# Two moves in GpSimd's hand-written order: one fold of each attention unit, and the addition to the sum over heads

## The chip, the cores and the metric

The kernel runs on one core of one Trainium2 chip. The metric is the device time of one execution in microseconds (us). Before the change three runs took 1590.33, 1591.95 and 1596.36 us; their median is 1591.95 us.

## What is computed

Two residual blocks over x of shape (2, 2048, 256), all in float32: first a layer norm and a recurrent network over the 2048 positions, then a layer norm and an attention with 8 heads of width 64, whose values and outputs are mixed from 5 experts by top-2 gates.

```python
x = x + rnn(layernorm(x))                       # h = tanh(x Wi + bi + h Wh + bh)
y = layernorm(x)
q, k = (y @ Wq), (y @ Wk)                       # 8 heads of 64
gl_v = (y @ Ws).reshape(b, t, h, e)
wv = topk_mask(gl_v, 2) * sigmoid(gl_v)
v = einsum('bthe,btek->bhtk', wv, einsum('btd,edk->btek', y, Wv))
probs = softmax(q * scale @ k^T)                # over 2048 keys
attn = einsum('bhij,bhjd->bihd', probs, v)
mask_o = topk_mask((y @ Wd).reshape(b, t, h, e), 2)
out = x + einsum('bthe,bthk,ekd->btd', mask_o, attn, Wo)
```

The last sum runs over heads and experts: each head adds its masked result to a sum `yd` in DRAM, and the product with Wo is made once for all heads.

## The kernel before

The first 190 us hold the recurrent block and the first layer norms. The rest is the attention, one long pipeline whose instruction order is written out by hand: it stands in a region of manual schedule, where each engine does its instructions in the order in which the Python code issues them.

The work is cut into 64 *units*: 2 batches x 8 heads x 4 blocks of 512 queries. A unit has eight tiles of keys, numbered 0 to 7 (variable `c`); a tile is 128 partitions (keys) x 2 x 512 (two groups of 128 keys by 512 queries), 512 KB. The main loop runs over 256 steps `T`; a unit takes `U_T` = 4 steps, two tiles each. A tile goes through these functions:

- `scores` (L636, TensorE): keys by queries into PSUM.
- `stage` (L648, ScalarE): copies the tile from PSUM to a buffer `p` of a ring; `largest` (L658, VectorE) takes the running maximum. The maximum over a unit's keys is turned, reduced and spread again (L677, L682, L691; `top`, L697).
- `subtract` (L704): subtracts that maximum, in place. Tiles 0 and 1 of a unit are done by VectorE, tiles 2 to 7 by GpSimd. It comes `LAG - 1` = 5 steps behind the scores.
- `exponential` (L707, ScalarE), in place. Of a step's two tiles one comes at the end of a step and the other at the start of the next.
- `products` (L717, TensorE): the tile by the values, into `o`, in step `T` for the tiles whose scores were made six steps before.
- `fold` (L729): a DMA that GpSimd issues and that adds the odd tile of a pair to the even one (`accum_op` add). It comes one step after the pair's products. It waits for these products, since it overwrites the even tile, and for the exponentials. A unit has four: of tiles 0, 2, 4 and 6.
- `sums` (L738, TensorE): adds up folded tiles against a column of ones, for the softmax's divisor. In step `T` with `T - LAG` odd; one call takes the folded tiles 0 and 2, the other, two steps later, 4 and 6. It is queued on TensorE behind the products of its step and ahead of the next step's scores.

When a unit is done, `take` and `take_sums` copy and add its results, `close` (L783, VectorE) makes `pro`, the unit's result for the five experts, and `gather` (L829 to L840) adds it to the sum over heads: for head 0 a store by SyncE (L835), for heads 1 to 6 a DMA with addition that GpSimd issues (L837), for head 7 an addition on GpSimd to a tile `y` that was loaded (L840). `pro` has one buffer.

What doesn't belong to the tiles of a step is put into tables by step, `before`, `first_behind` and `behind` (L939 to L1025). In the main loop (L1127 to L1173) a step issues, in this order: `take` and the exponential of an older tile, two score tiles with their staging and maxima, the subtractions and the fold, what `before` holds, the products, the sums, an exponential, and what `behind` holds. GpSimd's own order over a unit's four steps is thus:

- step with `T % 4 == 0`: subtract 6, fold of tile 2, subtract 7
- step with `T % 4 == 1`: fold of tile 4, and `gather` of an older unit (from `behind`)
- step with `T % 4 == 2`: subtract 2, fold of tile 6, subtract 3
- step with `T % 4 == 3`: subtract 4, fold of tile 0, subtract 5

`close` of the same older unit is in `behind` one step ahead of `gather`. SyncE issues the other transfers of the attention: among them the fetch of 640 KB of expert values for the next head (L608), the exchange of query halves (L170, L171), and in parts of the run loads of x, y and z.

Of the kernel before, what the change touches and what calls it, by code (L numbers as in the profile page):

```python
# [20 lines left out]
def rnn_then_switchhead_kernel(  # L21
# [16 lines left out]
    B, T, D = x.shape  # L38
    E, _, DH = Wv.shape
    H = Wq.shape[1] // DH  # L40
# [516 lines left out]
    U_T = NCH // 4  # L557
    LAG = U_T + 2
# [70 lines left out]
    def scores(t):  # L629
        i, n = units[t // HC]  # L630
        c = t % HC
        ss = ps_s.tile([P, 2, QB], F32, tag="s", name=f"s{t}")
        for o in range(2):
            half = slice(o * DH, (o + 1) * DH)
            for g in range(0, P, 32):
                nc.tensor.matmul(  # L636
                    ss[g : g + 32, o, :],
                    lhsT=k_of[i][half, c, g : g + 32],
                    rhs=q_of[i, n][o][half, :],
                    start=True,  # L640
                    stop=True,
                    tile_position=(o * DH, g),
                )
        return ss

    def stage(t, ss):
        p = ap.tile([P, 2, QB], F32, tag=f"p{t % 2}", bufs=RING[t % 2], name=f"p{t}")
        nc.scalar.copy(p, ss)  # L648
        ring[t] = p

    def largest(t, ss):

        u, c = t // HC, t % HC
        if c == 1:
            m_of[u] = ap.tile([P, 2, QB], F32, tag="mx", bufs=1, name=f"m{u}")
        m = m_of[u]
        if c != HC - 2:
            nc.vector.tensor_tensor(m, ss, ring[t - 1] if c == 1 else m, ALU.max)  # L658
            return
        half = misc([P, QB], f"mh{u}")  # L660
        nc.vector.tensor_tensor(half, ss[:, 0, :], m[:, 0, :], ALU.max)
        nc.vector.tensor_tensor(m[:, 1, :], ss[:, 1, :], m[:, 1, :], ALU.max)
        mm_of[u] = ap.tile([P, QB], F32, tag="mm", bufs=1, name=f"mm{u}")
        nc.vector.tensor_tensor(mm_of[u], half, m[:, 1, :], ALU.max)
        m_of.pop(u)
# [7 lines left out]
    def turn_max(u):  # L673
        pm = misc([P, QS, P], f"pm{u}")
        mm = mm_of.pop(u)
        for s in range(QS):
            nc.tensor.transpose(pm[:, s, :], mm[:, s * P : (s + 1) * P], ident)  # L677
        mx_of[u] = (pm, ap.tile([P, QS], F32, tag="mq", name=f"mq{u}"))

    def reduce_max(u):  # L680
        pm, mq = mx_of[u]
        nc.vector.tensor_reduce(mq, pm, AX.X, ALU.max)  # L682
# [16 lines left out]
    def subtract(t, on_vector=False):  # L699
        u, c = t // HC, t % HC  # L700
        p = ring[t]
        on_vector |= c < 2
        eng, top = (nc.vector, top_of[u][0]) if on_vector else (nc.gpsimd, top_of[u][1])
        eng.tensor_tensor(p, p, top.unsqueeze(1).to_broadcast([P, 2, QB]), ALU.subtract)  # L704

    def exponential(t):
        nc.scalar.activation(ring[t], ring[t], AF.Exp)  # L707

    def products(t):
        u, c = t // HC, t % HC  # L710
        i, _ = units[u]
        if c == 0:
            o_of[u] = ps_o.tile([P, QB], F32, tag="o", name=f"o{u}")
        for o in range(2):
            for g in range(0, DH, 32):
                at_col = o * DH + g
                nc.tensor.matmul(  # L717
                    o_of[u][at_col : at_col + 32, :],
                    lhsT=v_of[i][:, 2 * c + o, g : g + 32],
                    rhs=ring[t][:, o, :],  # L720
                    start=c == 0,
                    stop=c == HC - 1,
                    tile_position=(0, at_col),
                )

    def fold(t):


        nc.gpsimd.dma_start(out=ring[t], in_=ring.pop(t + 1), accum_op=ALU.add)  # L729

    def sums(t, t1, first, last):


        u = t // HC
        if first:
            den_of[u] = ps_o.tile([P, QB], F32, tag="d", name=f"d{u}")
        for g in range(4):
            nc.tensor.matmul(  # L738
                den_of[u][32 * g : 32 * (g + 1), :],
                lhsT=ones32,  # L740
                rhs=ring[(t, t1)[g // 2]][:, g % 2, :],
                start=first,
                stop=last,
                tile_position=(0, 32 * g),
            )
        ring.pop(t)
        ring.pop(t1)

    def take(u):

        o = o_of.pop(u)
        os = ap.tile([P, QB], F32, tag="os", bufs=1, name=f"os{u}")
        nc.scalar.copy(os[0:DH, :], o[0:DH, :])
        nc.vector.tensor_tensor(os[0:DH, :], o[DH:P, :], os[0:DH, :], ALU.add)  # L754
        o_of["s", u] = os
# [183 lines left out]
    before, first_behind, behind = {}, {}, {}  # L939

    def at(table, T, f, *a):
        table.setdefault(T, []).append(lambda: f(*a))
# [9 lines left out]
    for i, (b, h) in enumerate(heads):  # L952
# [11 lines left out]
        for part in range(4):  # L964
# [3 lines left out]
            else:  # L968
                T = T0 + U_T * (part - 2) + 2
# [3 lines left out]
        if h == H - 3 and b + 1 < B:  # L973
            for c in range(NCH):
                T = T0 + c // 2 * U_T + 1
                at(before if c % 2 else behind, T + c % 2, experts, b + 1, c)
    for b in range(1, B):

        T0 = (b - 1) * H * H_T + 2 * LAG + 3
        for c in range(NCH):  # L980
            T = T0 + c // 2 * U_T
# [6 lines left out]
        for c in range(NCH):  # L988
            T = T0 + c // 2 * U_T + c % 2
# [12 lines left out]
    for u, (i, n) in enumerate(units):  # L1002
        b, h = heads[i]
        T1 = (u + 1) * U_T
        if T1 < NT:
            at(first_behind, T1, spread_max, u)
        outs = [(b, n * QS + s) for s in range(QS)]
        if T1 + LAG < NT and h == H - 1:
            at(behind, T1 + LAG, fetch_y, u)
        if T1 + LAG + 1 < NT - 1:  # L1010
            at(behind, T1 + LAG + 1, take_sums, u)
            at(behind, T1 + LAG + 2, close, u)
            at(behind, T1 + LAG + 3, gather, u)
        if h == H - 1 and n < NQ - 3:
            T = T1 + LAG + 4
            for o, t, p in zip(outs, (0, 1, 3, 3), (1, 2, 3, 4)):
                if T + t < NT:
                    at(before if o[1] % QS == 2 else behind, T + t, turn_out, *o)
                if T + p < NT:
                    at(behind if o[1] % QS == 2 else before, T + p, project_out, *o)  # L1020
        if h == H - 1 and b < B - 1 and n >= NQ - 3:
            T = T1 + LAG + 4
            for o, t, p in zip(outs, (0, 1, 3, 3), (1, 2, 3, 4)):
                at(before if o[1] % QS == 2 else behind, T + t, turn_out, *o)
                at(behind if o[1] % QS == 2 else before, T + p, project_out, *o)  # L1025
# [100 lines left out]
    with tc.manual_schedule():  # L1126
        for T in range(NT):  # L1127
            new = (2 * T, 2 * T + 1)
            sub = [t for t in (2 * (T - LAG + 1), 2 * (T - LAG + 1) + 1) if 0 <= t < 2 * NT]
            old = [t for t in (2 * (T - LAG), 2 * (T - LAG) + 1) if 0 <= t < 2 * NT]  # L1130
            u_old = (T - LAG) // U_T - 1
            done = (T - LAG) % U_T == 0 and 0 <= u_old < len(units)
            fresh = sub and sub[0] % HC == 0
            if done:
                take(u_old)
            if old:
                exponential(old[1])

            ss = [scores(t) for t in new]
            stage(new[0], ss[0])  # L1140
            if T % U_T == 0:
                stage(new[1], ss[1])
                if T > 0:
                    turn_max(T // U_T - 1)
                    reduce_max(T // U_T - 1)
                largest(new[1], ss[1])
            else:
                largest(new[1], ss[1])
                stage(new[1], ss[1])
            if fresh:  # L1150
                subtract(sub[0])
            if T % U_T:
                largest(new[0], ss[0])
            if fresh:
                subtract(sub[1])
            if sub and not fresh:
                subtract(sub[0])
            k = T - LAG
            if k > 0:
                fold(2 * (k - 1))  # L1160
            if sub and not fresh:
                subtract(sub[1])
            for f in before.pop(T, []):
                f()
            for t in old:
                products(t)
            if 3 <= k and k % 2:
                t = 2 * (k - 3)
                sums(t, t + 2, t % HC == 0, t % HC != 0)
            if sub:  # L1170
                exponential(sub[0])
            for f in first_behind.pop(T, []) + behind.pop(T, []):
                f()  # L1173
        assert not before and not behind and not first_behind
        scores_only.close()
        spare["pool"] = ctx.enter_context(tc.tile_pool(name="ps_z", bufs=4, space=PSUM))
        drain()
# [46 lines left out]
```

## Time and profile before

| | |
|---|---|
| median of three runs | 1591.95 us |
| the profiled execution's own time | 1591.29 us |
| its span in the profile | 1589.5 us |
| TensorE clock granted | 0.996 |
| DMA moved | 254.09 MB, of it 164.65 MB by GpSimd's queue |
| fold DMAs (L729) | 254, 512 KB each, 6.6 us (median) from issue to landing |
| additions to yd by GpSimd (L837) | 48, 640 KB each, 7.6 us |
| fetches xq (L608) | 60, 640 KB each, 5.8 us |

Times in the profile are microseconds from the span's start. A group of instructions reads: line, engine, operation, output and input tile with shapes, count, then total busy time and the mean in ns of one, then the engine's idle time just ahead of the group and what ended most of it. A line of the waits reads: waiting engine, tile and line, what it waited for, then total, number of times, longest. PE is TensorE's matmuls, PEld its weight loads, DVE VectorE, ACT ScalarE, POOL GpSimd, SP SyncE. A line of the timeline reads: start, duration, instruction, count, and in brackets the idle time ahead of it with what ended it.

### The profile page before, as it was taken

What the parts mean: (1) busy time and instruction counts of PE and PEld (TensorE: products, weight loads), DVE (VectorE), ACT (ScalarE), POOL (GpSimd) and SP (SyncE); (2) the same over time, 40 slices, a digit from 0 to 9 for tenths busy, and PEclk for the clock granted to TensorE, in tenths of its full rate; (3) what the DMA queues carried; (4) which work ended last, traced back from release to release, by engine and by line L of the source; (5) the groups of instructions that cost most, each with busy time, mean ns of one, the idle gap of its engine ahead of it and who ended that gap; (6) DMA issues with size and microseconds to landing.
All of it is one profiled execution on the core that took longest, in us unless ns stands there. A gap on an engine that the chain in (4) does not pass through costs nothing. (4 is left out here: it accounts for less than half of the span.)

```text
span 1589.5 us, 41502 instructions
## 1 busy us (share of the span) xinstructions
PE 1529.4 (96%) x17582; PEld 542.1 (34%) x17582; DVE 1299.2 (82%) x1811; ACT 1248.1 (79%) x1617; POOL 1280.7 (81%) x855
## 2 busy tenths in 40 slices
PE   6989899999999999999999999999999999999997
PEld 5984222222233333333223332222222222222233
DVE  7473799999988878888987779989888888898883
ACT  4674688888888878888877678888888888888872
POOL 3053699888889987999997678898889889888880
PEclk9999999999999999999999999999999999999999
DMA  5021368898888888788886667888888888888855
GB/s 164 1 108 31 107 149 184 183 191 179 180 169 176 175 181 172 159 176 179 167 198 148 158 157 179 174 175 178 172 171 170 175 168 163 174 174 178 182 119 151
DMA packets 86959, 254.09 MB, mean 160 GB/s; under 512 B 11952, under 2 KB 31216, under 8 KB 86768
## 3 DMA queue, kind: packets, MB, share of 16 engines
q0 software_dynamic: 43488, 164.65, 55.5%
q1 hardware_dynamic: 41648, 86.13, 17.6%
q8 instruction: 139, 2.28, 0.6%
q10 hardware_dynamic: 1632, 0.61, 0.1%
q14 instruction: 52, 0.43, 0.1%
HBM read 59.46 MB, written 50.33 MB: 69 GB/s over the span
## 5 line engine op out<-in xcount | busy, mean ns | idle before, releaser
L704 POOL TENSOR_TENSOR p<-p,top 128x1024 f32<-128x1024 f32 x378 | 1051.4, 3017 | 10.7 <-ACT top L697 10.7
L648 ACT COPY p<-s 128x1024 f32<-128x1024 f32 x512 | 511.2, 1012 | 155.2 <-DVE m L658 63.3
L707 ACT ACTIVATE p<-p 128x1024 f32<-128x1024 f32 x512 | 538.5, 1063 | 51.3 <-DVE p L704 40.8
L636 PE MATMUL s<-q,k 64*32 64x512 f32 x4096 | 497.5, 596 | 2.8 <-ACT p L648 2.4
L636 PE MATMUL s<-qs,k 64*32 64x512 f32 x4096 | 497.3, 596 | 2.9 <-ACT p L648 1.9
L717 PE MATMUL o<-p,v 128*32 128x512 f32 x4096 | 491.1, 597 | 2.4 <-DVE os L754 1.5
L658 DVE TENSOR_TENSOR m<-s,m 128x1024 f32<-128x1024 f32 x320 | 390.5, 1220 | 108.0 <-PE s L636 99.6
L729 POOL DMA_DIRECT2D p<-p x254 | 346.2, 1364 | 53.3 <-ACT p L707 19.8
L717 PEld LDWEIGHTS o<-p,v 128*32 128x32 f32 x4096 | 113.7, 109 | 298.5 <-issue 157.2
L738 PE MATMUL d<-p,ones 128*32 128x512 f32 x1032 | 156.1, 594 | 8.6 <-DMA p<-p 8.6
L636 PEld LDWEIGHTS s<-qs,k 64*32 64x32 f32 x4096 | 102.6, 106 | 151.5 <-issue 56.7
L636 PEld LDWEIGHTS s<-q,k 64*32 64x32 f32 x4096 | 102.6, 106 | 147.8 <-issue 59.2
L704 DVE TENSOR_TENSOR p<-p,pt 128x1024 f32<-128x1024 f32 x126 | 152.3, 1209 | 0.0
L658 DVE TENSOR_TENSOR m<-s,p 128x1024 f32<-128x1024 f32 x64 | 78.4, 1224 | 57.3 <-ACT p L648 56.8
L837 POOL DMA_DIRECT2D yd<-pro x48 | 44.7, 931 | 90.0 <-DVE pro L783 87.8
L783 DVE TENSOR_TENSOR pro<-po,mr 128x1280 f32<-128x1280 f32 (+1 forms) x67 | 95.9, 1431 | 2.7
L620 DVE TENSOR_TENSOR xq<-xq,wp 128x1280 f32<-128x1280 f32 x60 | 89.2, 1487 | 2.3 <-DVE wp L618 0.3
L626 DVE TENSOR_REDUCE v<-xq 128x256 f32<-128x1280 f32 x60 | 88.6, 1476 | 0.0
L738 PEld LDWEIGHTS d<-p,ones 128*32 128x32 f32 x1032 | 38.0, 110 | 102.6 <-issue 74.8
L159 PE MATMUL pq<-xn2T,wq 128*32 128x512 f32 x512 | 63.2, 612 | 6.3 <-DVE rootd L425 6.3
L140 PE MATMUL pk<-xn2T,wk 128*32 128x512 f32 x512 | 61.5, 598 | 0.0
L396 POOL TENSOR_TENSOR x<-x,hvb 128x512 f32<-128x512 f32 x14 | 17.9, 1277 | 45.8 <-ACT hs L369 34.2
(179 smaller groups left out, 1511.0 us busy)
## 6 DMA issues: line engine op xcount, KB each, us to landing
p<-p POOLq DMA_DIRECT2D x254, 512.0 KB, 6.6
xq<-xvd SPq DMA_DIRECT2D x60, 640.0 KB, 5.8
yd<-pro POOLq DMA_DIRECT2D x48, 640.0 KB, 7.6
qs<-q SPq DMA_DIRECT2D x64, 128.0 KB, 3.3
yd<-pro SPq DMA_DIRECT2D x8, 640.0 KB, 5.3
y<-yd SPq DMA_DIRECT2D x8, 640.0 KB, 7.7
x<-in_x SPq DMA_DIRECT2D x16, 256.0 KB, 5.7
x1d<-x SPq DMA_DIRECT2D x16, 256.0 KB, 2.0
```

The source lines that it names most:

```text
L159: nc.tensor.matmul(pq[at_col : at_col + 32, :], lhsT=wq[:, kc, h * DH + g : h * DH + g + 32], rhs=xn2T[:, kc, b, n * QB : (n + 1) * QB], s ...
L620: nc.vector.tensor_tensor(xq, xq, wp.unsqueeze(2).to_broadcast([P, 4, DH, E]), ALU.mult)
L626: nc.vector.tensor_reduce(v_of[i][:, 4 * part : 4 * part + 4, :], xq, AX.X, ALU.add)
L636: nc.tensor.matmul(ss[g : g + 32, o, :], lhsT=k_of[i][half, c, g : g + 32], rhs=q_of[i, n][o][half, :], start=True, stop=True, tile_positi ...
L648: nc.scalar.copy(p, ss)
L658: nc.vector.tensor_tensor(m, ss, ring[t - 1] if c == 1 else m, ALU.max)
L704: eng.tensor_tensor(p, p, top.unsqueeze(1).to_broadcast([P, 2, QB]), ALU.subtract)
L707: nc.scalar.activation(ring[t], ring[t], AF.Exp)
L717: nc.tensor.matmul(o_of[u][at_col : at_col + 32, :], lhsT=v_of[i][:, 2 * c + o, g : g + 32], rhs=ring[t][:, o, :], start=c == 0, stop=c == ...
L729: nc.gpsimd.dma_start(out=ring[t], in_=ring.pop(t + 1), accum_op=ALU.add)
L738: nc.tensor.matmul(den_of[u][32 * g : 32 * (g + 1), :], lhsT=ones32, rhs=ring[(t, t1)[g // 2]][:, g % 2, :], start=first, stop=last, tile_ ...
L783: nc.vector.tensor_tensor(dst, po[:, s : s + n, 0:DH].unsqueeze(2).to_broadcast([P, n, E, DH]), mr[:, s : s + n].unsqueeze(3).to_broadcast ...
```

## The change

The diff touches two places. In the tables, `gather` of every head but the last is put one step later, into the step with `T % 4 == 2`, where it comes behind that step's two subtractions and its fold. In the main loop, in steps with `T % 4 == 0`, the fold (of tile 2) is issued ahead of both subtractions and not between them. Other steps keep their order.

```diff
         if T1 + LAG + 1 < NT - 1:
             at(behind, T1 + LAG + 1, take_sums, u)
             at(behind, T1 + LAG + 2, close, u)
-            at(behind, T1 + LAG + 3, gather, u)
+            at(behind, T1 + LAG + 3 + (h < H - 1), gather, u)
...
             if fresh:
                 subtract(sub[1])
+            k = T - LAG
+            first = T % U_T == 0
+            if first and k > 0:
+                fold(2 * (k - 1))
             if sub and not fresh:
                 subtract(sub[0])
-            k = T - LAG
-            if k > 0:
+            if not first and k > 0:
                 fold(2 * (k - 1))
             if sub and not fresh:
                 subtract(sub[1])
```

GpSimd's order over a unit's four steps becomes:

- `T % 4 == 0`: fold of tile 2, subtract 6, subtract 7
- `T % 4 == 1`: fold of tile 4 (and `gather` if the older unit is of head 7)
- `T % 4 == 2`: subtract 2, fold of tile 6, subtract 3, `gather`
- `T % 4 == 3`: subtract 4, fold of tile 0, subtract 5

The first move concerns 62 folds, the second the `gather` of 56 units: 48 DMAs of GpSimd and 8 stores of SyncE. The orders of TensorE, VectorE and ScalarE are the same as before. SyncE's eight stores of head 0 come behind the loads and query exchanges of the step that they are moved to.

## The prediction

> **What bounds the kernel now.** I read the page's busy shares first, then the groups, the list of waits, and the timelines of two neighbouring units on TensorE and on GpSimd (POOL). A unit is four steps; its key tiles are 0 to 7. I write S2 to S7 for the six subtractions that GpSimd does (L704), F0, F2, F4, F6 for its four fold DMAs (L729), G for the addition to the sum over heads (L837, a DMA).
>
> ```profile
> PE 1529.4 (96%) x17582; PEld 542.1 (34%) x17582; DVE 1299.2 (82%) x1811; ACT 1248.1 (79%) x1617; POOL 1280.7 (81%) x855
> ...
> L704 POOL TENSOR_TENSOR p<-p,top 128x1024 f32<-128x1024 f32 x378 | 1051.4, 3017 | 10.7 <-ACT top L697 10.7
> ...
> L729 POOL DMA_DIRECT2D p<-p x254 | 346.2, 1364 | 53.3 <-ACT p L707 19.8
> ...
> L738 PE MATMUL d<-p,ones 128*32 128x512 f32 x1032 | 156.1, 594 | 8.6 <-DMA p<-p 8.6
> ...
> L837 POOL DMA_DIRECT2D yd<-pro x48 | 44.7, 931 | 90.0 <-DVE pro L783 87.8
> ```
>
> TensorE is the bound, with nearly no idle time; GpSimd's one regular idle time is ahead of G. The waits add what the group of the sums hides:
>
> ```profile
> POOL yd L837 <- DVE pro L783: 87.8, 42, 3.3
> ...
> PEld d L738 <- DMA p<-p: 27.3, 34, 3.8
> ...
> PE d L738 <- DMA p<-p: 8.6, 7, 2.9
> ```
>
> 34 times TensorE's weight loads for the sums wait for a fold to land: 27.3 us, and the matmuls queued behind wait with them. The timeline of TensorE shows one unit with the wait and the next without it:
>
> ```profile
> 1124.93 1.03 PE L738 MATMUL d<-p,ones 128*32 128x512 f32 x4
> 1126.99 1.05 PE L738 MATMUL d<-p,ones 128*32 128x512 f32 x4 [1.03 <-DMA p<-p]
> 1127.97 0.63 PE L636 MATMUL s<-q,k 64*32 64x512 f32 x4
> ...
> 1146.97 1.04 PE L738 MATMUL d<-p,ones 128*32 128x512 f32 x8
> 1147.95 0.63 PE L636 MATMUL s<-qs,k 64*32 64x512 f32 x4
> ```
>
> With the wait, the first sums of a unit last 3.1 us (1124.93 to 1128.04), without it 1.04. These are the sums of tiles 0 to 3, and the later half needs F2. Reading the start of each unit's first L636 matmul in the trace, the unit with the wait is 22.03 us long and the next 20.29. In the second batch (26 units, 34 to 59), 11 units have no wait and last 20.29 or 20.30; the other 15 last 20.41 to 22.63. A unit's length is 20.29 plus its wait less about 0.32: the maximum of L658 in that step ends 0.3 us later than the sums would, and the next scores wait for that too. The excess over 20.29 adds up to 12.5 us.
>
> GpSimd's timeline over a unit boundary (step 0 of the new unit begins at 1158.31):
>
> ```profile
> 1154.24 1.47 POOL L729 DMA_DIRECT2D p<-p  x1
> 1154.85 5.63 POOL L704 TENSOR_TENSOR p<-p,top 128x1024 f32<-128x1024 f32 x2
> 1159.57 1.76 POOL L729 DMA_DIRECT2D p<-p  x1
> 1160.18 3.56 POOL L704 TENSOR_TENSOR p<-p,top 128x1024 f32<-128x1024 f32 x1
> 1162.51 2.07 POOL L729 DMA_DIRECT2D p<-p  x1
> 1166.27 0.87 POOL L837 DMA_DIRECT2D yd<-pro  x1 [1.69 <-DVE pro L783]
> ```
>
> These are F0, S5 and S6, F2, S7, F4, G. F2 is issued at 1159.57, though its last condition (the products of tiles 2 and 3, ended 1157.5) was met 2 us before: S6 stands ahead of it. Lastly the landing of single folds (DMA issues of L729 in narrow windows), for the F2 of the unit with the wait and of the one without:
>
> ```profile
> DMA to landing us min/median/max: 9.7/9.7/9.7
> ...
> DMA to landing us min/median/max: 5.6/5.6/5.6
> ```
>
> The first was issued at 1117.23, 1.0 us ahead of SyncE's fetch of 640 KB (L608, 1118.20), the second at 1138.54, 1.7 us ahead of it (1140.24).
>
> **What the Trainium skill says.** "Perfetto Trace Analysis", Identifying the Most-Contended Engine: matmul busy time does not tell how near TensorE is to its limit. The trace agrees: PE shows 8.6 us of idle time ahead of the sums, the unit lengths 12.5 us in one batch alone. The same page, DMA Instruction — SWDGE (GPSIMD): a GpSimd DMA's record ends when descriptors are generated, not when data is there. It agrees: record 1.8 us, landing 9.7. "DMA: Bandwidth & Descriptors", Two DMAs through the same engine are not ordered: within one queue descriptors start in order; and its Queues, rings and completion order: an engine alternates between queues packet by packet. So F2 waits for what GpSimd issued before it, and shares with SyncE's transfers from then on; the two landings fit.
>
> **The change part by part.** Instructions, durations and the orders of TensorE, VectorE and ScalarE stay.
>
> F2 ahead of S6, 62 times. GpSimd gives S6 and S7 0.61 us less time early (from F2's start to the next start, 1159.57 to 1160.18) and gets it back before S7. New order here: F2 waits for the products, 1157.2 to 1157.5 (folds start up to 0.3 us before the modelled end of the products), instead of 1159.57: 2.1 to 2.4 us earlier. The added wait holds S6 and S7. S6 then starts at 1158.1 at most (before: 1157.2) and takes 3.0: ends 1161.1; ScalarE takes it 4.26 us into the unit, 1162.6. Cover 1.5 us. S7 starts 2.36 later (S6 follows S5 by that in the trace, as no DMA stands between), 1160.5, ends 1163.5 to 1163.8; it ended 1163.74 before, and its exponential starts at 1164.0. Cost nothing, with 0.2 to 0.5 us of cover, and 1.3 us more (median of the trace) from that exponential's end to its product on TensorE.
>
> F2's landing. SyncE's fetch would now follow 3 us behind F2, not 1 to 1.7, so I take 5.6 us: landed at 1163. With the bad 9.7 it lands at 1167.1; the later half of the sums wants it at 9.5 us into the unit, 1167.8. The wait goes either way.
>
> G behind S2, F6, S3, 48 times (head 7's addition, L840, stays where it is). Its wait (1.9 us a unit, 87.8 in all) is gone, since pro is long done by then; GpSimd was ahead by that much, so this is not 87.8 us of time. It buys S2 to S5 an earlier start, and so F2's issue never slips past the products as it did in units 24 and 28 (S5 ended 0.8 and 2.2 us after the unit began; in 28 this cost 1.4 us of TensorE through S7). It adds 0.57 us ahead of S4, whose exponential comes 3.8 us after S4's end (median): covered. The next pro needs the buffer some 15 us after the new G; G lands in 7.6 (median). The eight stores of head 0 (L835) move on SyncE's queue the same way, past loads that are wanted two steps or more later: nothing.
>
> The GpSimd queue's order becomes F4, F6, G, F0, F2. Issue times in the 20.29 us unit before, from its start (1138.01): F4 4.1, G 8.0, F6 10.9, F0 16.2, F2 21.6, next F4 24.5, gaps from 2.9 to 5.4. After, each fold at the end of its products: F4 4.2, F6 8.9, G 12 (behind S3), F0 15.5, F2 19.3, next F4 24.5, gaps from 3.1 to 5.2, and F2 no longer has the next F4 2.9 us behind it. Unproven is F2 with G and F0 in front: low cost nothing, high a landing of 11 us or more. I take none, as G and F0 have 7 us to pass before F2 is issued.
>
> Sum: second batch 12.5 us; first batch 13 units with waits of 11.4 us in all, 7.3 if each is discounted 0.32; the longest ones (1.97, 3.90) show in full in the unit's length, so 9; unit 28 1.4. Together 22.9, less 1.5 for the 3.90, where two fetches of 640 KB stand beside F2 and some wait stays: 21.5. Against the profiled execution: 1591.3 (span 1589.5 and 1.8 around it) to 1569.8; it stands 0.7 under the median of 1591.95, so 1570.5 as a median. What is late next is L658's maximum in the same step: already in the 0.32.
>
> **The rivals.** Partly: in the first batch other work (experts, gates) fills the same place, and only the second gains, 1591.95 - 12.5 = 1579.5. For: units there last 20.7 to 24 us. Against: their waits show in full. No gain: G and F0 ahead in the queue delay F2's data by as much as it is earlier (2.3 us), 1592. For: the DMA engines are 83% busy in these stretches. Against: the gaps above. Slower, at the same place: F2's landing takes over 10.7 us (0.9 earlier than the unit's start, 9.5 into it, 0.3 of cover); each us beyond costs about 60 units x 1 us, against today's 22, so it decides from 11.1 us; at 11.5 it is 48 - 22 = 26 us, 1618. For: single folds took 12.3. Against: F2's median is 7.3 today, in the same traffic.
>
> **How the numbers follow.** Forecast 0.68 (1563 to 1577), partly 0.15, no gain 0.11, slower 0.06. Range 1563 to 1584: forecast and nearly all of partly. 0.5% (8 us) is what a measurement can tell from no change: below 1584 0.82, within 0.12, above 0.06.
>
> **What would show it.** The wait of the sums for p<-p falls from 27.3 to under 5 us, units of the second batch last 20.3, POOL's wait for pro is gone and waits of L729 for the products appear. Wrong: waits for p<-p as before with a later landing, or ScalarE waiting for L704.

## The result, and the profile after

The changed kernel takes 1570.73 us (median of 6 runs, 1568.86 to 1573.80); six runs of the kernel before have a median of 1593.18 us. The ratio is 0.986, 95% interval 0.984 to 0.988. The profiled execution's span fell from 1589.5 to 1567.6 us.

The page after, for the busy shares and the groups that were shown of before:

```profile
PE 1512.6 (96%) x17582; PEld 533.7 (34%) x17582; DVE 1299.1 (83%) x1811; ACT 1247.8 (80%) x1617; POOL 1287.7 (82%) x855
...
L704 POOL TENSOR_TENSOR p<-p,top 128x1024 f32<-128x1024 f32 x378 | 1006.3, 2768 | 27.9 <-ACT top L697 27.4
...
L729 POOL DMA_DIRECT2D p<-p x254 | 263.0, 1036 | 97.6 <-issue 42.4
...
L738 PE MATMUL d<-p,ones 128*32 128x512 f32 x1032 | 135.0, 592 | 0.9 <-DMA p<-p 0.9
...
L837 POOL DMA_DIRECT2D yd<-pro x48 | 61.0, 1270 | 0.0
```

Busy time of VectorE and ScalarE is what it was. The sums (L738) have lost 21 us, from 156.1 to 135.0, though no matmul was taken out, and the mean record stayed at 592 to 594 ns. The records of the eight matmuls lie over one another when nothing waits (x8 in 1.04 us, in the prediction's lines); when the later four wait for F2, they come as two halves of 1.03 and 1.05 us, one behind the other. So part of a wait shows as busy time. The addition to yd (L837) has lost its idle time of 90.0 us; GpSimd now idles ahead of subtractions (27.9 us, for the maximum) and of folds (97.6 us, where it was 53.3). It is idle in other places, and is not what got faster.

Who waits for a fold, from the profile's view of line 729 (waiting engine, us, times):

```profile
  PEld d L738: 1.8, 1
  PE d L738: 0.9, 1
...
DMA to landing us min/median/max: 4.5/5.4/11.9
```

27.3 us in 34 waits have become 1.8 in one. A fold lands 5.4 us after its issue (median), before 6.6. GpSimd's timeline over the same unit boundary as in the prediction (here the unit begins at 1146.10):

```profile
1137.60 1.21 POOL L837 DMA_DIRECT2D yd<-pro  x1
1138.23 3.01 POOL L704 TENSOR_TENSOR p<-p,top 128x1024 f32<-128x1024 f32 x1
1141.29 0.88 POOL L729 DMA_DIRECT2D p<-p  x1
1141.90 2.70 POOL L704 TENSOR_TENSOR p<-p,top 128x1024 f32<-128x1024 f32 x1
1145.02 0.88 POOL L729 DMA_DIRECT2D p<-p  x1 [0.42 <-issue]
1145.64 5.02 POOL L704 TENSOR_TENSOR p<-p,top 128x1024 f32<-128x1024 f32 x2
1150.32 1.18 POOL L729 DMA_DIRECT2D p<-p  x1
```

These are G, S4, F0, S5, F2, S6 and S7, F4. F2 is issued 1.08 us ahead of the unit; before it was 1.26 behind. The 0.42 us ahead of it, named "issue", is the wait for the products: 57 of the 64 folds of tile 2 start 0.27 to 0.29 us before their modelled end.

Unit lengths, from the first L636 matmul of each unit (a unit is numbered here by the sums that fall into it, and begins with the first scores of the next unit but one): in the second batch, 25 of 26 units last 20.30 or 20.31 us (before: 20.29 to 22.63). Both batches were added up against the kernel before: the 26 units of the second are 12.6 us shorter, the 34 of the first 8.4. That is 21.0 of the span's 21.9; the rest lies ahead of the units (1.2 us shorter) and behind them (0.3 us longer).

### The profile page after: what moved, and what is told of

Same layout as the page of the kernel before. It is cut to its first block, busy times and chain, and to the rows that moved or that the text cites. A ratio compares the mean times of both kernels' runs of the same rounds, so it can differ in the third digit from the quotient of the medians.

```text
span 1567.6 us, 41503 instructions
## 1 busy us (share of the span) xinstructions
PE 1512.6 (96%) x17582; PEld 533.7 (34%) x17582; DVE 1299.1 (83%) x1811; ACT 1247.8 (80%) x1617; POOL 1287.7 (82%) x855
## 5 line engine op out<-in xcount | busy, mean ns | idle before, releaser
L704 POOL TENSOR_TENSOR p<-p,top 128x1024 f32<-128x1024 f32 x378 | 1006.3, 2768 | 27.9 <-ACT top L697 27.4
L636 PE MATMUL s<-q,k 64*32 64x512 f32 x4096 | 501.6, 596 | 3.6 <-ACT p L648 2.4
L636 PE MATMUL s<-qs,k 64*32 64x512 f32 x4096 | 501.4, 596 | 3.3 <-ACT p L648 1.8
L729 POOL DMA_DIRECT2D p<-p x254 | 263.0, 1036 | 97.6 <-issue 42.4
L636 PEld LDWEIGHTS s<-qs,k 64*32 64x32 f32 x4096 | 100.3, 105 | 154.6 <-ACT p L648 58.2
L636 PEld LDWEIGHTS s<-q,k 64*32 64x32 f32 x4096 | 100.2, 105 | 153.9 <-ACT p L648 59.9
L738 PE MATMUL d<-p,ones 128*32 128x512 f32 x1032 | 135.0, 592 | 0.9 <-DMA p<-p 0.9
L837 POOL DMA_DIRECT2D yd<-pro x48 | 61.0, 1270 | 0.0
L738 PEld LDWEIGHTS d<-p,ones 128*32 128x32 f32 x1032 | 33.9, 110 | 77.8 <-issue 75.8
```

The costliest lines, as they stand in the source:

```text
L636: nc.tensor.matmul(ss[g : g + 32, o, :], lhsT=k_of[i][half, c, g : g + 32], rhs=q_of[i, n][o][half, :], start=True, stop=True, tile_positi ...
L738: nc.tensor.matmul(den_of[u][32 * g : 32 * (g + 1), :], lhsT=ones32, rhs=ring[(t, t1)[g // 2]][:, g % 2, :], start=first, stop=last, tile_ ...
```

## The experiments

Theory A: the time is set by when F2 lands, against the moment at which the sums want it, and that depends on whether F2 is ahead of SyncE's fetch. Theory B: the gain is GpSimd's time, freed by the wait for pro. Theory C: each move has its own share, and they add up. The kernel before, timed beside them, had medians of 1593.28 us (first four kernels) and 1591.99 (last two).

**The first move alone.** The changed kernel with the addition to yd back in its old step:

```diff
-            at(behind, T1 + LAG + 3 + (h < H - 1), gather, u)
+            at(behind, T1 + LAG + 3, gather, u)
```

> Only the first move: the fold of tile 2 goes ahead of subtractions 6 and 7; the addition to yd stays where it was, with its wait for pro. Theory A (the time is set by when that fold lands, against the 9.5 us into the unit at which the sums want it): the fold is issued about 1 us before the unit's start, 3 us ahead of the fetch, lands by 6, the waits of the sums for p<-p fall under 5 us though GpSimd still waits some 85 us for pro; 1573 us (1569 to 1578). Theory B (the gain is the GpSimd time freed by the wait for pro): no change, 1590 to 1595. Theory C (each move has a share of its own and the shares add up): about half, 1578 to 1586.

Measured: 1572.33 us, ratio 0.986 (0.984 to 0.988). The lists of waits of this kernel, for the sums and for the addition:

```profile
PEld d L738 <- DMA p<-p: 3.1, 5, 1.5
...
POOL yd L837 <- DVE pro L783: 75.0, 42, 2.9
```

GpSimd still waits 75 us for pro, and the gain is there all the same. Theory B falls. A's number was 1573.

**The second move alone.** The kernel before with one edit; the fold stays between subtractions 6 and 7:

```diff
-            at(behind, T1 + LAG + 3, gather, u)
+            at(behind, T1 + LAG + 3 + (h < H - 1), gather, u)
```

> Only the second move: the addition to yd comes a step later, behind the subtractions; the fold of tile 2 stays between subtractions 6 and 7. Theory A: GpSimd comes to subtraction 6 early in every unit, so the fold is issued 0.5 us into each unit as in those units of before that had no wait, 1.7 us ahead of the fetch, and lands by 7.6: the waits for p<-p fall under 5 us, 1573 us (1569 to 1579), about as much as with the first move alone, so the two shares do not add up. Theory B: the whole gain, 1570.7. Theory C: about half, 1578 to 1586.

Measured: 1576.39 us, ratio 0.989 (0.987 to 0.991), and for the sums:

```profile
PEld d L738 <- DMA p<-p: 6.3, 6, 4.4
```

The second batch gains the whole 12.6 us: in nearly every unit S6 starts early, F2 is issued 0.5 us into the unit and lands by 6.0 to 6.8 (in one unit 1.2 and 7.9). The waits are a little over the 5 us that were expected. The first batch gains 3.2 of 8.4, since unit 29, near which SyncE fetches y twice (L804), waits 4.4 us (with both moves 1.8). The moves do not add up (21.0 alone, 16.9 alone, 22.5 together, each as the difference of medians): each brings F2 ahead of the fetch, and that can be done once. C falls. What the second move adds to the first, 1.6 us, is within the intervals and is not shown.

**The fold behind both subtractions.** The kernel with the second move alone, and the fold still later:

```diff
             if sub and not fresh:
                 subtract(sub[0])
             k = T - LAG
-            if k > 0:
+            first = T % U_T == 0
+            if not first and k > 0:
                 fold(2 * (k - 1))
             if sub and not fresh:
                 subtract(sub[1])
+            if first and k > 0:
+                fold(2 * (k - 1))
```

> The second move with the fold of tile 2 behind both subtractions. Theory A: the fold is issued about 3.2 us into the unit, 1 us behind the fetch of 640 KB, lands at 11.7 to 13, and the sums wait 1.9 to 3.2 us beyond their cover in some 55 units: 1690 us (1640 to 1740), waits for p<-p over 100 us. Theory B: the wait for pro is gone all the same, 1571.

Measured: 1592.69 us, ratio 0.999 (0.998 to 1.001). Sums:

```profile
PEld d L738 <- DMA p<-p: 32.1, 30, 4.1
```

All of the gain is lost again, so B is wrong here too; but the waits are 32 us and not over 100, and my 1690 was far off. F2 is issued 2.9 us into the unit, yet lands at 8.5 to 9.0 in the units without a wait, mostly 5.8 us after its issue. In the other units of the second batch it lands as late as 10.7 (in one 13.1); why was not followed. I had added a late landing of before, 9.7, to a later issue. That landing was not a property of the fold: it contained a wait for the fetch to go by. The next paragraph shows it.

**What a late fold waits for.** Two windows of 2.6 us in the trace of the kernel before, each in the same place of a unit: the queues that moved data (packets, MB, share of 16 engines). First the unit with the late landing, whose F2 was issued at 1117.23 and whose fetch was issued at 1118.20, from 1119.1 to 1121.7:

```profile
q1 hardware_dynamic: 87, 0.45, 93.2%
```

Then the unit with the early landing (F2 at 1138.54, fetch at 1140.24), from 1140.3 to 1142.9:

```profile
q0 software_dynamic: 109, 0.45, 107.5%
```

In each there is one data queue only: q1 is SyncE's, q0 GpSimd's. The transfer whose first packet came first has the engines to itself in these windows, and the other's first packet comes 2.8 to 3.0 us later. It is not so in every unit. In unit 49 the two first packets are 1.0 us apart, and from 1265.7 to 1268.7 both queues move data:

```profile
q1 hardware_dynamic: 82, 0.42, 36.0%
q0 software_dynamic: 79, 0.32, 65.3%
```

From the packet records and the landings, in us from the unit's start ("record ends" is the end of F2's instruction on GpSimd):

| | F2 issued | record ends | F2's first packet | fetch's first packet | F2 landed |
|---|---|---|---|---|---|
| before, unit 43 | 0.52 | 1.66 | 2.23 | 5.19 | 6.12 |
| before, unit 42 | 1.25 | 3.03 | 6.01 | 3.18 | 10.97 |
| before, unit 49 | 0.80 | 2.39 | 2.96 | 3.94 | 9.53 |
| fold behind both, unit 44 | 2.87 | 4.00 | 5.07 | 3.18 | 8.69 |
| changed kernel, unit 44 | -1.08 | -0.20 | 0.38 | 3.23 | 3.62 |
| tile 0 on GpSimd (last experiment), unit 43 | -0.12 | 3.16 | 5.58 | 3.75 | 9.73 |

The last row shows that the time of issue, at which the record starts, does not decide by itself. In the kernel before, F2's record ends 0.84 us after the end of the subtraction ahead of it in all 26 units of the second batch, whenever it started, and F2's first packet comes 0.57 us after the record's end in the 12 of them in which the fetch is not ahead. The fetch's comes 0.95 us after its issue if F2 is not ahead, 3.18 us into the unit. So F2 should be first if its record ends before 3.18 - 0.57 = 2.61 us. In the second batches of the kernel before, of the second move alone and of tile 0 on GpSimd that holds for all 78 folds of tile 2: where the record ended by 2.54 us, the first packet came by 3.7; where it ended at 2.60 or later, at 5.6 or later. Once F2 has lost, it hardly matters when it was issued: 1.25 and 2.87 give first packets at 6.01 and 5.07. That is why the cost has a step and is nearly flat behind it.

**The fetch moved away.** GpSimd's order of before; VectorE's sum over experts is done a step earlier, so that the fetch's buffer is free earlier:

```diff
-                at(before, T + 1, mix_sum, i, part)
+                at(behind, T, mix_sum, i, part)
```

> GpSimd's order is that of the kernel before. VectorE's sum of the mixed experts (L626) is done right behind the mixing, one step earlier, so that the buffer of the fetch (L608) comes free in the step with T % 4 == 2 or 3 and the fetch no longer runs beside the fold of tile 2. Theory A with the fetch as what makes the late folds land late: issue of the fold as before (0.5 to 1.3 us into the unit), landing in about 5.6 us and not 9.7, waits for p<-p under 5 us; 1572 us if VectorE's new order costs nothing, up to 1590 if it delays its maxima by 0.3 us a unit. Rival: GpSimd's own DMAs, issued close behind, are what delays it; then landing stays at 8 to 10 us for the late ones and the waits for p<-p stay over 20 us, time 1590 or more.

Measured: 1605.46 us, ratio 1.008 (1.005 to 1.010). The sums' wait:

```profile
PEld d L738 <- DMA p<-p: 3.9, 4, 2.3
```

The wait is gone with no change in GpSimd's order, though GpSimd still waits 98.7 us for pro. The fetch is issued 2.2 us ahead of the unit in nearly all units of the second batch and has landed by 3.3 in 24 of these 26. F2 lands 5.6 us after its issue (median over all units), before 7.3. But in this batch F2's record also ends earlier in the unit, at 2.4 us at the latest, where the late kind of before ended at 2.70 to 3.03; by the 2.61 us of above F2 would have been ahead of a fetch in its old place too. Four units of the first batch (15, 17, 22, 26) separate the two causes: the record ends at 2.54 to 3.19 us, no earlier than before (2.48 to 3.02), and the next fold is issued at most 0.2 us later than before. F2's first packet now follows the record's end by 0.57 us and not by 3.0 to 3.2, and F2 lands at 6.3 to 6.9 us and not at 9.2 to 9.6. So the fetch it was, and not GpSimd's own DMAs behind F2. The rest of my number was wrong: VectorE's new order costs not 0 to 0.3 us a unit but 0.77 (21.07 against 20.30), and TensorE now waits 12.7 us in 47 waits for the last part of the maximum (before: 1.1 us in 4):

```profile
PEld s L636 <- DVE m L662: 12.7, 47, 0.3
```

How the moved sum brings about the whole 0.77 was not followed further.

**Is GpSimd's new idle time worth anything?** In the changed kernel GpSimd waits some 1.5 us in most units of the second batch. Two kernels give it a seventh subtraction, of tile 0 or of tile 1, both built on the changed kernel and with the fold of tile 4 ahead of it:

```diff
-        on_vector |= c < 2
+        on_vector |= c == 1
...
+            k = T - LAG
+            first = T % U_T < 2
+            if first and k > 0 and fresh:
+                fold(2 * (k - 1))
             if fresh:
                 subtract(sub[0])
...
-            k = T - LAG
-            first = T % U_T == 0
-            if first and k > 0:
+            if first and k > 0 and not fresh:
                 fold(2 * (k - 1))
```

This is the kernel with tile 0; for tile 1 VectorE keeps `c == 0`, and the fold stands ahead of the second subtraction.

> The changed kernel, and GpSimd takes over the subtraction of tile 0 as well (tile 1 stays with VectorE); the fold of tile 4 is issued ahead of it. In the changed kernel a unit of the second batch lasts 20.30 us, GpSimd waits some 1.9 us of it, and the second scores of step 2 start 0.05 us behind VectorE's maximum of tile 2, which stands behind the subtraction of tile 0. Theory A (the next limit is that maximum): it comes 1.1 us earlier, the scores of step 2 up to 0.3 us a unit, so 1555 us (1550 to 1565), with the exponential of tile 0 no longer waiting for VectorE. Rival (GpSimd becomes the bound): its seven subtractions at 2.36 us, four folds at 0.61 and the addition at 0.57 are 19.5 us of 20.3, any wait for the products or for the maximum then makes it late, the exponentials wait for GpSimd: 1575 to 1600, with waits of L707 for POOL over 10 us.

> As the one before, but GpSimd takes over tile 1 and VectorE keeps tile 0: the same load on GpSimd, while the maximum of tile 2 stays where it was. Theory A: nothing to gain in step 2, 1570 us (1566 to 1576). Rival (GpSimd the bound): as with tile 0, 1575 to 1600. If both come out alike below 1565, neither is right and the time freed on VectorE at large is what counts.

Measured: 1610.69 us, ratio 1.012 (1.009 to 1.014), with tile 0, and 1612.24 us, ratio 1.012 (1.010 to 1.015), with tile 1. ScalarE's wait and GpSimd's group in the kernel with tile 0:

```profile
ACT p L707 <- POOL p L704: 106.5, 163, 2.8
```

```profile
L704 POOL TENSOR_TENSOR p<-p,top 128x1024 f32<-128x1024 f32 x441 | 1284.7, 3901 | 11.3 <-ACT top L697 11.3
L729 POOL DMA_DIRECT2D p<-p x254 | 586.8, 2315 | 27.3 <-ACT p L648 7.4 <-issue 5.6 <-ACT k L148 5.3
```

The rival is right in kind, and the time lies above its 1600: the exponentials wait for GpSimd 163 times. The sums also wait for folds again, 21.7 us in 24 waits with tile 0, since F2's record ends behind the 2.6 us of above in half of the units of the second batch. In the mean a unit of that batch takes 20.92 us. The starts of GpSimd's instructions add up to only 19.5, and the profile shows hardly any idle time of GpSimd ahead of them, as the records overlap: the mean record of a subtraction is 3.9 us where it was 2.8, that of a fold 2.3 where it was 1.0. The missing time is a wait all the same. From GpSimd's and ScalarE's timelines:

```profile
1171.95 3.27 POOL L729 DMA_DIRECT2D p<-p  x1
...
1177.26 3.54 POOL L729 DMA_DIRECT2D p<-p  x1
1179.27 6.27 POOL L704 TENSOR_TENSOR p<-p,top 128x1024 f32<-128x1024 f32 x2
...
1177.65 1.06 ACT L707 ACTIVATE p<-p 128x1024 f32<-128x1024 f32 x1 [0.23 <-POOL p L704]
1178.62 0.56 ACT L697 COPY top<-pt 128x512 f32<-128x512 f32 x1
```

The first line is F2 of unit 43, in the table above. The subtraction of tile 0 starts 2.0 us after the fold ahead of it (F4) and not 0.6, and 0.09 us after the end of ScalarE's copy of the maximum (`top`). It starts 0.09 us behind that copy in all 26 units of the batch. The copy stands in ScalarE's order behind an exponential that has just waited for GpSimd: GpSimd is late for ScalarE, and ScalarE then for GpSimd. So the idle time that the change gave GpSimd is slack that the order needs, not room for one more instruction.

On the next limit the unit lengths say something. With tile 0 on GpSimd nine of the 26 units last 19.98 or 19.99 us, with tile 1 none is shorter than 20.30. That fits the 0.3 us a unit that theory A gave an earlier maximum of tile 2, in the units where GpSimd keeps up; most others lose more than that.

## Why the prediction was right

**The sum.** 21.5 us were forecast (the terms add up to 21.4), 22.5 came as the difference of medians. That the forecast 1570.5 lies 0.2 us beside the measured median is luck, as single runs spread over 5 us and the forecast started 1.2 us lower, from the median of three runs; the batches are the better test: 12.5 forecast and 12.6 measured in the second; 9 and 1.4 less 1.5 forecast, 8.9 in all, and 8.4 measured in the first. The 1.5 us left for unit 29 were 1.8. Unit 28 gained 0.8 and not 1.4. The 0.32 us by which I discounted a wait was too much: unit 42 of before waits 1.94 us and is 1.74 longer than its shortest neighbours, a discount of 0.2.

**F2 ahead of S6.** Forecast: issued 0.8 to 1.1 us ahead of the unit, S6 ended 2.8 us into it at most, S7 at 5.2 to 5.5. Measured: 1.08 ahead, S6 at 2.23, S7 at 4.56, its exponential at 5.69. The added wait holds S6 as expected and its cover was larger than worked out: S5 had ended earlier, so that F2 waited for the products with an empty queue ahead, and two subtractions with no DMA between them take 5.02 us.

**F2's landing.** I took 5.6 us and 9.7 at worst; the median is 5.3. The step holds, but its reason was half right. I took it that F2 and SyncE's transfers share the engines packet by packet. In unit 49 of before both queues do move data in one window, but the two windows above show 2.6 us of one queue alone. A fold has 128 data packets in the trace and 16 closing ones, so 8 data packets an engine if there is one closing packet for each; the engines may still alternate, in pieces as large as that. No run here tells. I also took the time of issue for the one that counts, where the end of the record decides. So the forecast feared a slow decline where there is a step, and the changed kernel is far from it: in the second batch its record ends at the unit's start at the latest, against 2.6. The first error is also why my number for the fold behind both subtractions failed.

**G behind the subtractions.** Its 87.8 us of waiting are gone and were, as said, no time of their own: the first move gives 21.0 us with 75 us of that wait still there. But I gave the second move too little. It would have removed nearly all the waits of the second batch by itself, because S6 ends 1.3 us earlier in the units that had waited (0.84 and not 2.17 us into unit 44), and so F2's record ends ahead of the fetch.

**The rivals.** Partly (1579.5): the first batch did gain. No gain (1592): the gaps between GpSimd's DMAs were wide enough; F4 and F6 land earlier too (medians 5.3 and 4.8 us from issue, before 7.3 and 7.4), and F0, which now has G ahead of it, only 0.5 us later (6.1), with some 6 us or more to spare before its sums in the second batch. Slower (1618): in the second batch F2 lands between 3.5 and 6.7 us into the unit, the point from which it decides is 9.8. Moving the fold the other way showed that even a landing behind the fetch only takes the gain back.

## What to carry to other kernels

A wait that is short on average can be a matter of either or: here the units whose fold came behind the fetch lost 0.1 to 2.3 us, all others nothing, but for one that lost 0.3. Look at such a wait unit by unit, look at the end of a DMA's record on GpSimd and not only at its start, and ask what a DMA with a late landing was waiting for, before you add that landing to another issue time. If two edits each bring the same transfer ahead of the same rival, expect the gain once. And idle time of a queue that is worked in order is not free room: what GpSimd gained here could not be filled with one more subtraction, and where records overlap, a wait between two starts shows as no idle time at all.

## What was not expected of the hardware

Two DMA queues kept apart for 2.6 us while both had data to move: 87 packets of SyncE's queue and no data packet of GpSimd's, and in the next unit 109 of GpSimd's and none of SyncE's, decided by whose first packet was earlier. It is no general rule, as unit 49 shows both in one window. What keeps the second back is not settled; no run here tells whether it is the engines or the making of the descriptors.

When a GpSimd DMA can start to move data, at the earliest, is told by its record's end and not by the start: 0.56 to 0.59 us from the end to the first packet in all 26 units of the second batch with the second move alone, while the time from the start was 1.68 to 2.08 us there and up to 3.92 with tile 0 on GpSimd.
